# A graph layer's edge sums on one core: shorter packing sums, a share of the gathers fetched row by row from two hardware queues, PSUM copies moved to VectorE

## The chip, the cores and the metric

The kernel runs on one core of a Trainium2 chip, as a single program. The metric is the device time of one execution in microseconds. A profile is one further execution, recorded by the hardware profiler; its span runs from the first to the last instruction.

Engines are named as in the profile: PE (TensorE), PEld (its weight loads), DVE (VectorE), ACT (ScalarE), POOL (GpSimd), SP (SyncE). "SPq" and "ACTq" are what the sequencers of SP and ACT do themselves, issuing transfers and loading registers.

## The reference, cut to what matters

A layer over a graph of 50,000 nodes and 1,650,000 edges (src, dst), sorted by dst. Each node has 160 float32 features, each edge four numbers. Every node also has an edge to itself.

```python
ss, vv = s[src], v[src]                    # the features of the source node of each edge: 64 + 32 x 3
dot  = einsum('eui,ei->eu', vv, e1)
out0 = C0 * (ss * e0 @ W1 + dot * INV3 @ W2)
...
m     = concatenate([out0, out1], 1)       # a message for each edge
m_agg = segment_sum(m, dst, n)             # summed at the target node
h     = [m_agg_s @ Ws, m_agg_v @ Wv]       # 160 features again
y     = x + relu(h)
out   = layernorm(x + y)
```

All of a message is linear in (edge number k) x (source feature). So the kernel sums, for each target node and each k, the source rows weighted by the edge's number k, and applies the weights afterwards, per node.

## The kernel before, in words

**Units, groups, pairs.** 128 edges are a unit. G = 6 units are a group; as the edges are sorted by dst, the targets of a group lie in a window of W = 32 nodes. For a unit, POOL gathers the 128 source rows from HBM with one indirect DMA into a tile `xg` (`gather`, pool `rows`, six buffers). DVE builds from the targets a one-hot matrix `hot` and multiplies it by the four edge numbers to `ha`, 128 edges x (4 x 32) (`spread`). PE multiplies the two into PSUM `ps` (`group_sums`), six units per group. PG = 2 groups are a pair, and the main loop runs over the 1,050 pairs. SG = 20 groups are a superchunk: src, dst and the edge numbers of the next one are fetched (`load`), converted to float (`cast`) and transposed by PE (`place`) while the present one is worked on.

**After the sums.** Four groups are a chunk: `turn` transposes its sums on PE and copies them out of PSUM (`at`), `apply_weights` multiplies by the folded weights (`hp`), and `nodes`, `block` and `norm1` to `norm3` add up the chunks of 128 nodes, add x, normalize and store `out`. Copies from PSUM go through a name `evict`, which is ACT's copy here. These steps are put into the main loop a few pairs after the sums that they need (`after_pair`).

**Packing.** Each node has an edge to itself, so about one edge in 33 needs no gather from far: its source row lies in the group's own window. For 1,980 of the 2,100 groups (all but a head of NH = HEAD = 100 groups and a rest of 20), a group spans L = 787 edges, and K = 19 edges that loop onto their own node are taken out, so that 768 remain to be gathered. `pack` does this for RP = 120 groups at a time, one group per partition, with DVE:
- it marks the self edges (`m`), numbers them (`cum`) and computes how far each later edge moves up (`far`),
- it sums, for each window node w and edge number k, what the self edges carry (`waste`, with the sum in `mine`): 2 halves x 4 x 32 instructions over some 393 columns each,
- it moves the edges up in steps of 1, 2, 4, 8, 16, with predicated copies, and stores the result to HBM (`sd`, `ad`), from where `load` reads it.

`pack` is a generator: a step is taken at each pair, so that the work is spread up to the pair by which it must be done. What the self edges carry is added in `group_sums`: `own` fetches the 32 rows of the group's window four times over (`xo`, a transfer at an address loaded into a register), and DVE adds xo x `taken` to `ps` on its way to `A`.

**Fetching by rows.** The code has a second way to fill a unit, switched off in this kernel (`HELP = {}`). `fetch` loads row addresses (`offsets`, from a tile `ro`) into registers of SP or ACT and issues one transfer of 640 bytes for each row, into a tile `xr` (pool `far`, three buffers for each queue). `HELP` gives for each queue the number of units out of which it takes one. `batches` spreads the 128 rows in batches of ROWS over the pairs, the last two pairs ahead of their use; `gather` leaves out the units so filled, which come last in their pair.

**Queues.** SP's queue issues all loads and `own`; ACT's queue issues the weights and the stores of `out`.

Of the kernel before, what the change touches and what calls it, by code (L numbers as in the profile page):

```python
# [44 lines left out]
P = 128  # L45
# [17 lines left out]
HELP = {}  # L63
HEAD = 100
RP = 120
ROWS = 32
# [28 lines left out]
def tile_gnn_resnorm(ctx: ExitStack, tc: tile.TileContext, x, src, dst, attr, W1, W2, W3, W4, W5, Ws, Wv, out, n_edges):  # L95
# [92 lines left out]
    def norm3(pool, y, mv, rstd, n, row):  # L188
        nc.vector.reciprocal(rstd[:n], rstd[:n])  # L189
        o = pool.tile([P, D], F32, name="o")  # L190
        nc.vector.tensor_scalar(o[:n], y[:n], mv[:n, 0:1], rstd[:n], op0=ALU.subtract, op1=ALU.mult)  # L191
        nc.scalar.dma_start(out[row, :], o[:n])
# [18 lines left out]
    with tc.tile_pool(name="once", bufs=1) as once, tc.tile_pool(name="raw", bufs=2) as rawp, \  # L211
            tc.tile_pool(name="idx", bufs=2) as idxp, tc.tile_pool(name="rows", bufs=6) as rowp, \
            tc.tile_pool(name="far", bufs=3) as farp, tc.tile_pool(name="own", bufs=4) as ownp, \
# [13 lines left out]

        offsets = {}
        evict = nc.vector.tensor_copy if ET.Activation in HELP else nc.scalar.copy

        def load(s):
# [4 lines left out]
            if NH <= g0 < NH + NPK:  # L236
                sd, ad = stored[(g0 - NH) // RP]
                e = slice((g0 - NH) % RP * G * P, ((g0 - NH) % RP * G + n) * P)
                rf = rawp.tile([P, 2, P], F32, name="rf")
                for i in range(2):  # L240
                    nc.sync.dma_start(rf[:n, i, :], sd[i:i + 1, e].rearrange("o (u p) -> (o u) p", p=P))
                nc.sync.dma_start(ra[:n].rearrange("u p k -> u (p k)"), ad[e].rearrange("(u p) k -> u (p k)", p=P))
                return s, n, None, rf, ra
            e = slice(start(g0), start(g0) + n * P)
            ri = rawp.tile([P, 2, P], I32, name="ri")
            nc.sync.dma_start(ri[:n, 0, :], src1[e].rearrange("(u p) o -> u (p o)", p=P))
            nc.sync.dma_start(ri[:n, 1, :], dst1[e].rearrange("(u p) o -> u (p o)", p=P))
            nc.sync.dma_start(ra[:n].rearrange("u p k -> u (p k)"), attr[e].rearrange("(u p) k -> u (p k)", p=P))
# [55 lines left out]

        def own(p):

            s, g, ng = pairs[p]
            if not NH <= g < NH + NPK:
                return
            _, at = nc.values_load_multi_w_load_instructions(  # L310
                baseO[0:1, g:g + ng], engines=[ET.SP], min_val=0, max_val=(N - W) * 4 * D,
                skip_runtime_bounds_check_because="an offset of a row of x")
            xo = ownp.tile([P, PG, D], F32, name="xo")
            for i, v in enumerate(at):
                nc.sync.dma_start(xo[:, i, :].bitcast(U8),
                                  xbytes[ds(v, W * 4 * D)].rearrange("(w f) -> w f", w=W).unsqueeze(0)
                                  .to_broadcast([NK, W, 4 * D]))
# [20 lines left out]
        owns, stored, taken = {}, {}, {}  # L338
        halves = ((0, L // 2), (L // 2, L))

        def pack(c):
# [9 lines left out]
            nc.sync.dma_start(pri[:n, 0, :], src1[e].rearrange("(r e) o -> r (e o)", e=L))  # L351
            nc.sync.dma_start(pri[:n, 1, :], dst1[e].rearrange("(r e) o -> r (e o)", e=L))
            nc.sync.dma_start(pra[:n].rearrange("r e k -> r (e k)"), attr[e].rearrange("(r e) k -> r (e k)", e=L))
            nc.sync.dma_start(pb[:n], base_d[NH + r0:NH + r0 + n])
            yield
            nc.scalar.copy(prs[:n], pri[:n])
# [3 lines left out]
            cum = packp.tile([P, L], F32, name="cum")  # L360
            far = packp.tile([P, L], I32, name="far")
            less = packp.tile([P, L], I32, name="less")
            carry = packp.tile([P, 1], F32, name="carry")
            pbf = packp.tile([P, 1], F32, name="pbf")
            mine = packp.tile([P, 2, NK * W], F32, name="mine")
            waste = packp.tile([P, L], BF16, name="waste")
            nc.vector.tensor_scalar(pbf[:n], pb[:n], float(N - W), None, op0=ALU.min)
            for h, (a, e) in enumerate(halves):
                q = slice(0, e - a)
                nc.vector.tensor_tensor(m[:, q], prs[:n, 0, a:e], prs[:n, 1, a:e], op=ALU.is_equal)  # L370
                nc.vector.tensor_tensor_scan(cum[:n, a:e], m[:, q], zeros[:n].to_broadcast([n, e - a]),
                                             carry[:n] if h else 0.0, op0=ALU.add, op1=ALU.add)
                nc.vector.tensor_copy(carry[:n], cum[:n, e - 1:e])
                yield

                nc.vector.scalar_tensor_tensor(m[:, q], cum[:n, a:e], float(K), m[:, q], op0=ALU.is_le, op1=ALU.mult)
                nc.vector.tensor_scalar(cum[:n, a:e], cum[:n, a:e], float(K), None, op0=ALU.min)
                nc.vector.scalar_tensor_tensor(far[:n, a:e], m[:, q], 0.0, cum[:n, a:e],
                                               op0=ALU.is_equal, op1=ALU.mult)
                yield  # L380
                nc.vector.tensor_scalar(cum[:n, a:e], prs[:n, 1, a:e], pbf[:n], None, op0=ALU.subtract)
                nc.vector.tensor_reduce(packed[:n, 0, 2 * c + h:2 * c + h + 1], cum[:n, a:e], axis=AX.X, op=ALU.min)
                nc.vector.tensor_reduce(packed[:n, 1, 2 * c + h:2 * c + h + 1], cum[:n, a:e], axis=AX.X, op=ALU.max)

                nc.vector.scalar_tensor_tensor(m[:, q], cum[:n, a:e], 1.0, m[:, q], op0=ALU.add, op1=ALU.mult)
                yield
                for k in range(NK):
                    for w in range(W):
                        nc.vector.scalar_tensor_tensor(waste[:n, a:e], m[:, q], float(w + 1), pra[:n, a:e, k],  # L389
                                                       op0=ALU.is_equal, op1=ALU.mult,  # L390
                                                       accum_out=mine[:n, h, k * W + w:k * W + w + 1])
                        if w % 4 == 3:
                            yield
            nc.vector.tensor_copy(counts[:n, c:c + 1], carry[:n])
# [6 lines left out]
            for b in range(K.bit_length()):  # L401
                d = 1 << b
                for a, e in halves:
# [3 lines left out]
                    if d * 2 <= K:  # L407
                        nc.vector.tensor_scalar(less[:n, a:e + d], far[:n, a:e + d], 0x7fffffff - d, None,
                                                op0=ALU.bitwise_and)
# [8 lines left out]
                    yield  # L418
            sd = dram.tile([2, n * G * P], F32, name=f"sd{c}")
            ad = dram.tile([n * G * P, NK], F32, name=f"ad{c}")  # L420
            for i in range(2):
                nc.sync.dma_start(sd[i:i + 1].rearrange("o (r e) -> (o r) e", e=G * P), prs[:n, i, :G * P])
            nc.sync.dma_start(ad.rearrange("(r e) k -> r e k", e=G * P), pra[:n, :G * P])
# [37 lines left out]
        def nodes(b):  # L461
# [4 lines left out]
            nc.sync.dma_start(xt[:nb], x[row, :])  # L466
# [20 lines left out]
        nbatch = P // ROWS  # L487
        batches, helped = {}, {}
        for h, (eng, period) in enumerate(HELP.items()):
            first = PG * G + h * period // 2  # L490
            while True:
# [13 lines left out]
        def fetch(p):  # L505
            for eng, h, q, s, u, i in batches.get(p, []):
                if i == 0:
                    fetched[q, h] = farp.tile([P, D], F32, name=f"xr{h}")
                xr = fetched[q, h]
                _, at = nc.values_load_multi_w_load_instructions(  # L510
                    offsets[s][u:u + 1, i * ROWS:(i + 1) * ROWS], engines=[eng], min_val=0, max_val=(N - 1) * 4 * D,
                    skip_runtime_bounds_check_because="an offset of a row of x")
                for j, v in enumerate(at):
                    r = i * ROWS + j
# [7 lines left out]
        with nc.allow_non_contiguous_dma(reason="one number of each group"):  # L522
            for g0, g1, size in ((0, NH, G * P), (NH, NH + NPK, L), (NH + NPK, NGP, G * P)):
                if g0 < g1:
                    e = slice(start(g0), start(g0) + (g1 - g0) * size)
                    nc.sync.dma_start(base_d[g0:g1], dst1[e].rearrange("(g e) o -> g (e o)", e=size)[:, 0:1])
        baseI = baseB.bitcast(I32)
        nc.sync.dma_start(baseI, base_d.rearrange("g o -> o g").to_broadcast([P, NGP]))
# [4 lines left out]
        zeros = once.tile([P, 1], F32, name="zeros")  # L533
        nc.vector.memset(zeros, 0.0)
# [3 lines left out]
        packed = once.tile([P, 2, max(2 * npacks, 1)], F32, name="packed")  # L538
# [19 lines left out]
        hps, parts, of_nodes, resid, rstds = {}, {}, {}, {}, {}  # L558
# [15 lines left out]
        def do_store(b):  # L574
            norm3(np_, *resid.pop(b), rstds.pop(b), *rows_of(b))
# [245 lines left out]
```

## Time and profile before

| what | value |
|---|---|
| time before, median of 3 runs | 15,898.52 us (15,871.31 to 15,898.71) |
| time of the profiled execution | 15,879.8 us |
| span of the profiled execution | 15,878.0 us |
| mean granted TensorE clock | 0.648 of full speed |
| POOL busy | 11,926.1 us, 75% |
| PE busy, PE weight loads | 11,902.0 us, 75%; 8,781.1 us, 55% |
| DVE busy | 7,960.7 us, 50% |
| ACT busy | 897.9 us, 6% |
| moved by DMA | 1,382 MB, 87 GB/s |

A row of the groups reads: line, engine, operation, out<-in with shapes, count, then busy time in us and mean ns of one, then the engine's idle time just before these instructions, and what ended most of it. "issue" there means that nothing that the profile shows was waited for. Register loads and moves and the issuing of transfers are not counted as busy; the view of a single line gives their durations as min/median/max in ns.

### The profile page before, as it was taken

Reading aid. Unit: us, or ns where it says so; the run is one execution under the profiler, and the core shown is the slowest. Engines: PE = TensorE matmul, PEld = TensorE weight load, DVE = VectorE, ACT = ScalarE, POOL = GpSimd, SP = SyncE. Lnnn points to the kernel's source line nnn. Section 1 sums busy time; section 2 is a strip of 40 time slices with the busy share of each in tenths; the row PEclk is TensorE's granted clock in tenths of the full one; section 3 lists DMA queues with packets and bytes.
Section 4 is the critical chain, followed back from the end, with each engine's and each line's share of the span. In section 5 each row is a group of like instructions: output and inputs, shape, how many; then the busy total and the mean of one; then the engine's idle time right before and its main releaser. Section 6 shows DMA issues by size and latency. Waiting matters only on the chain. (4 is left out here: it accounts for less than half of the span.)

```text
span 15878.0 us, 132047 instructions
## 1 busy us (share of the span) xinstructions
PE 11902.0 (75%) x43059; PEld 8781.1 (55%) x43060; DVE 7960.7 (50%) x17460; ACT 897.9 (6%) x2069; POOL 11926.1 (75%) x12611
## 2 busy tenths in 40 slices
PE   7677777777777777777777777777777777777777
PEld 4455555555555555555555555555555555555555
DVE  4565555545454554545454554545455454545422
ACT  0000000000000000000000000000000000000000
POOL 7677777777777777777777777777777777777776
PEclk7666666666666666666666666666666666666666
DMA  3333333333333333333333333333333333333332
GB/s 83 74 86 94 84 82 96 82 95 84 94 83 92 85 82 96 83 96 83 94 85 87 91 82 96 84 94 84 94 83 82 96 82 96 83 93 84 86 83 70
DMA packets 1040422, 1382.05 MB, mean 87 GB/s; under 512 B 233153, under 2 KB 813393, under 8 KB 1035641
## 3 DMA queue, kind: packets, MB, share of 16 engines
q0 software_dynamic: 604800, 1033.00, 26.9%
q1 hardware_dynamic: 378065, 307.98, 7.1%
q10 hardware_dynamic: 56864, 32.58, 0.7%
q8 instruction: 344, 5.64, 0.1%
q14 instruction: 349, 2.86, 0.1%
HBM read 1303.90 MB, written 68.75 MB: 86 GB/s over the span
## 5 line engine op out<-in xcount | busy, mean ns | idle before, releaser
L288 POOL DMA_INDIRECT xg<-in_x,si x12600 | 11924.5, 946 | 3917.0 <-issue 3527.0
L325 PE MATMUL ps<-xg,ha 128*128 128x160 f32 x25200 | 8037.7, 447 | 3686.5 <-DMA xg<-in_x,si 3640.6
L325 PEld LDWEIGHTS ps<-xg,ha 128*128 128x128 f32 x25200 | 5302.5, 266 | 6227.7 <-DMA xg<-in_x,si 6033.2
L334 DVE SCALAR_TENSOR_TENSOR A<-xo,taken,ps 128x160 f32<-128x160 f32 x1980 | 728.8, 377 | 7231.3 <-PE ps L325 7231.3
L389 DVE SCALAR_TENSOR_TENSOR waste<-marks,pra 120x393 bf16<-120x393 f32 (+3 forms) x4352 | 3652.5, 839 | 2.9
L300 DVE TENSOR_TENSOR ha<-hot,pk 128x1536 f32<-128x1536 f32 x1050 | 1830.2, 1744 | 284.1 <-PE ps L325 284.0
L480 PE MATMUL phb<-hp,hot 128*128 128x160 f32 x4544 | 1181.0, 433 | 56.2 <-ACT at L439 52.8
L480 PEld LDWEIGHTS phb<-hp,hot 128*128 128x128 f32 x4544 | 1066.4, 297 | 173.3 <-ACT at L439 172.2
L436 PE MATMUL pt<-ident,A 128*128 128x128 f32 (+1 forms) x4200 | 1051.7, 406 | 100.1 <-ACT hp L454 67.8
L450 PE MATMUL phc<-BWb,at 32*128 32x160 f32 x4200 | 1078.0, 404 | 0.0
L439 ACT COPY at<-pt 128x512 f32<-128x512 f32 (+1 forms) x1050 | 596.9, 579 | 6815.1 <-PE pt L436 6746.4
L450 PEld LDWEIGHTS phc<-BWb,at 32*128 32x128 f32 x4200 | 835.0, 253 | 196.3 <-issue 196.1
L450 PE MATMUL phc<-BWa,at 128*128 128x160 f32 x4200 | 922.6, 374 | 2.3 <-ACT at L439 2.0
L436 PEld LDWEIGHTS pt<-ident,A 128*128 128x128 f32 (+1 forms) x4200 | 700.7, 178 | 302.7 <-ACT hp L454 143.1
L450 PEld LDWEIGHTS phc<-BWa,at 128*128 128x128 f32 x4200 | 847.0, 255 | 35.3 <-ACT at L439 35.3
L297 DVE TENSOR_TENSOR hot<-bank,rel 128x384 f32<-128x384 f32 x1050 | 569.6, 544 | 0.3
L454 ACT COPY hp<-phc 128x160 f32<-128x160 f32 x525 | 153.3, 292 | 6230.2 <-PE phc L450 6171.5
L470 DVE TENSOR_TENSOR hot<-bank,rr 128x768 f32<-128x768 f32 (+2 forms) x391 | 358.8, 918 | 0.1
L389 DVE DVE_READ_ACCUMULATOR waste<-marks,pra 120x1 f32 (+1 forms) x4352 | 342.9, 79 | 0.0
L416 DVE COPY_PREDICATED pra<-marks,pra 120x1572 f32<-120x1572 int32 (+6 forms) x170 | 323.5, 1903 | 0.0
L176 DVE SCALAR_TENSOR_TENSOR y<-phb,xt 128x160 f32<-128x160 f32 x391 | 120.6, 308 | 195.6 <-PE phb L480 195.3
L414 DVE COPY_PREDICATED prs<-marks,prs 120x393 f32<-120x393 int32 (+6 forms) x340 | 181.3, 582 | 0.1
(98 smaller groups left out, 1610.1 us busy)
## 6 DMA issues: line engine op xcount, KB each, us to landing
xg<-in_x,si POOLq DMA_INDIRECT x12600
xo<-in_x SPq DMA_DIRECT2D x1980, 80.0 KB
xt<-in_x SPq DMA_DIRECT2D x390, 80.0 KB
out<-o ACTq DMA_DIRECT2D x390, 80.0 KB
ra<-ad SPq DMA_DIRECT2D x99, 240.0 KB
pra<-in_attr SPq DMA_DIRECT2D x16, 1475.6 KB
ad<-pra SPq DMA_DIRECT2D x16, 1440.0 KB
rf<-sd SPq DMA_DIRECT2D x198, 60.0 KB
```

The source lines that it names most:

```text
L288: nc.gpsimd.indirect_dma_start(out=xg[:, j, :], out_offset=None, in_=x, in_offset=bass.IndirectOffsetOnAxis(ap=placed[0][:, u + j:u + j + ...
L297: nc.vector.tensor_tensor(hot[:, :n], slotsP[:, 0:W].unsqueeze(1).to_broadcast([P, n, W]), rel[:, u:u + n].unsqueeze(2).to_broadcast([P, n ...
L300: nc.vector.tensor_tensor(ha[:, :n], hot[:, :n].unsqueeze(2).to_broadcast([P, n, NK, W]), pk[:, :, u:u + n].rearrange("p k u -> p u k").un ...
L325: nc.tensor.matmul(ps[:, j // G, :], ha[:, j].rearrange("p k w -> p (k w)"), xr, start=j % G == 0, stop=j % G == G - 1)
L334: nc.vector.scalar_tensor_tensor(A[:, i], xo[:, i], taken[r // RP][:, r % RP:r % RP + 1], ps[:, i], op0=ALU.mult, op1=ALU.add)
L389: nc.vector.scalar_tensor_tensor(waste[:n, a:e], m[:, q], float(w + 1), pra[:n, a:e, k], op0=ALU.is_equal, op1=ALU.mult, accum_out=mine[:n ...
L416: nc.vector.copy_predicated(pra[:n, a:e], mi[:, r].unsqueeze(2).to_broadcast([n, e - a, NK]), pra[:n, a + d:e + d])
L436: nc.tensor.transpose(pt[:f1 - f0, g, :], A[:, i, f0:f1], ident)
L439: evict(at[:, :, :ng].rearrange("f k g w -> f g k w"), pt[:f1 - f0, :ng].rearrange("f g (k w) -> f g k w", w=W))
L450: nc.tensor.matmul(ph[:ng * W], at[:, k, :ng].rearrange("f g w -> f (g w)"), bw[:, k, :], start=i == 0, stop=i == 2 * NK - 1)
L470: nc.vector.tensor_tensor(hot2[:, :len(cs)], slotsP.unsqueeze(1).to_broadcast([P, len(cs), P]), rr[:, :len(cs)].unsqueeze(2).to_broadcast( ...
L480: nc.tensor.matmul(ph[:nb], hot2[:r, i, :nb], hp[:r], start=i == 0, stop=i == len(cs) - 1)
```

## The change

Constants: `HELP` is switched on, SP takes one unit in 45 in batches of 32 rows, ACT's queue one in 90 in batches of 16; HEAD goes from 100 to 60, so that 2,020 groups are packed. With ACT in HELP, `evict` becomes DVE's copy. With SP in HELP, everything that SP issued before is issued by ACT's queue (`dq`), so that SP issues rows alone; `own` loads the addresses of five pairs at a time, and has five buffers. The store of `out` becomes a step of its own, a pair after its computation. In `pack`, the sum for window node w runs over those columns alone in which the targets of w can lie (L = 787 edges, 33 to a node; `early` and `late` are six standard deviations, and two checks are added at the end that no self edge lies outside); some tensor_scalar operations are replaced by forms with one operand in PSUM or two tensors; and there are empty steps after its loads and ahead of its stores. The program has 2,856 such sums in place of 4,352.

```diff
-HELP = {}
-HEAD = 100
+HELP = {ET.SP: 45, ET.Activation: 90}
+HEAD = 60
-ROWS = 32
+ROWS = {ET.SP: 32, ET.Activation: 16}
...
-            tc.tile_pool(name="far", bufs=3) as farp, tc.tile_pool(name="own", bufs=4) as ownp, \
+            tc.tile_pool(name="far", bufs=3) as farp, tc.tile_pool(name="own", bufs=5) as ownp, \
...
+        own_eng = ET.Activation if ET.SP in HELP else ET.SP
+        dq = nc.scalar if ET.SP in HELP else nc.sync
         offsets = {}
         evict = nc.vector.tensor_copy if ET.Activation in HELP else nc.scalar.copy
...
-                    nc.sync.dma_start(rf[:n, i, :], sd[i:i + 1, e].rearrange("o (u p) -> (o u) p", p=P))
+                    dq.dma_start(rf[:n, i, :], sd[i:i + 1, e].rearrange("o (u p) -> (o u) p", p=P))
...
+        OWN = 5
         def own(p):
...
-            _, at = nc.values_load_multi_w_load_instructions(
-                baseO[0:1, g:g + ng], engines=[ET.SP], min_val=0, max_val=(N - W) * 4 * D,
+            if p % OWN == 0:
+                g1 = min(g + OWN * PG, NH + NPK)
+                _, at = nc.values_load_multi_w_load_instructions(
+                    baseO[0:1, g:g1], engines=[own_eng], min_val=0, max_val=(N - W) * 4 * D,
...
+        degree = n_edges / N
+        late = 6 * math.sqrt(L) + 2 * degree
+        early = -6 * math.sqrt(L)
...
-                nc.vector.tensor_scalar(cum[:n, a:e], cum[:n, a:e], float(K), None, op0=ALU.min)
...
-                for k in range(NK):
-                    for w in range(W):
-                        nc.vector.scalar_tensor_tensor(waste[:n, a:e], m[:, q], float(w + 1), pra[:n, a:e, k],
+                for w in range(W):
+                    w0 = max(a, math.floor(degree * w + early))
+                    w1 = min(e, math.ceil(degree * w + late) + 1)
+                    for k in range(NK if w0 < w1 else 0):
+                        nc.vector.scalar_tensor_tensor(waste[:n, w0:w1], m[:, w0 - a:w1 - a], float(w + 1), pra[:n, w0:w1, k],
                                                        op0=ALU.is_equal, op1=ALU.mult,
                                                        accum_out=mine[:n, h, k * W + w:k * W + w + 1])
...
-                        nc.vector.tensor_scalar(less[:n, a:e + d], far[:n, a:e + d], 0x7fffffff - d, None,
-                                                op0=ALU.bitwise_and)
+                        nc.vector.tensor_tensor(less[:n, a:e + d], far[:n, a:e + d], mi[:, 0:e + d - a],
+                                                op=ALU.subtract)
...
+            nr = ROWS[eng]
             _, at = nc.values_load_multi_w_load_instructions(
-                    offsets[s][u:u + 1, i * ROWS:(i + 1) * ROWS], engines=[eng], min_val=0, max_val=(N - 1) * 4 * D,
+                    offsets[s][u:u + 1, i * nr:(i + 1) * nr], engines=[eng], min_val=0, max_val=(N - 1) * 4 * D,
...
+        def do_send(b):
+            nb, row = rows_of(b)
+            dq.dma_start(out[row, :], outs.pop(b)[:nb])
...
                     after_pair(p + 6, do_store, b)
+                    after_pair(p + 7, do_send, b)
```

## The prediction

> **What bounds the kernel now.** I read the page's engine table first (POOL 75%, PE 75%, DVE 50%, ACT 6%: no verdict), then the costliest groups, then POOL's stretch of the timeline, because an engine that is busy 75% can still never rest.
>
> ```profile
> span 15878.0 us, 132047 instructions
> PE 11902.0 (75%) x43059; PEld 8781.1 (55%) x43060; DVE 7960.7 (50%) x17460; ACT 897.9 (6%) x2069; POOL 11926.1 (75%) x12611
> ...
> L288 POOL DMA_INDIRECT xg<-in_x,si x12600 | 11924.5, 946 | 3917.0 <-issue 3527.0
> L325 PE MATMUL ps<-xg,ha 128*128 128x160 f32 x25200 | 8037.7, 447 | 3686.5 <-DMA xg<-in_x,si 3640.6
> ```
>
> The first group: 12,600 gathers, 946 ns each, and of the 3,917 us idle before them 3,527 us are "issue": POOL waits for nobody. The second: PE's idle time ahead of the edge matmuls ends with the landing of those gathers. The timeline of POOL alone shows the beat:
>
> ```profile
> 8012.42 0.95 POOL L288 DMA_INDIRECT xg<-in_x,si  x1 [0.30 <-issue]
> 8013.68 0.95 POOL L288 DMA_INDIRECT xg<-in_x,si  x1 [0.30 <-issue]
> 8014.93 0.94 POOL L288 DMA_INDIRECT xg<-in_x,si  x1 [0.30 <-issue]
> 8016.17 0.95 POOL L288 DMA_INDIRECT xg<-in_x,si  x1 [0.30 <-issue]
> ```
>
> One gather starts every 1.25 us. The gathers run from 7.6 us (first start) to 15,842.8 us (last start). 12,599 steps of 1.25 us are 15,749 us, so 86 us are real stalls, the largest one of 36.4 us (POOL's wait for si, L273). The last 35 us are the end of the kernel. So **the time is 7.6 + 1.25 us a gather + 86 + 35**, and the profiled run (15,879.8 us, 1.8 us outside its span) lies 18.7 us below the median of the runs, 15,898.5 us.
>
> Who feeds the new work? SyncE and ScalarE's queue show in no busy row; the single-line views give what they issue:
>
> ```profile
> L310 SPq TENSOR_LOAD <-baseO x990: 640/975/3587, 46.0 to 15623.3; - x198
> ...
> L315 SPq MOVE xo<-in_x x1980: 29/38/38, 46.9 to 15637.6; - x198
> L315 SPq DMA_DIRECT2D xo<-in_x x1980: 547/585/708, 47.0 to 15637.7; - x198
> ```
>
> These are min/median/max in ns: loading two addresses into registers takes 975, moving one into place 38, issuing the transfer of 128 rows 585. Between them the queue's timeline has gaps of 30 and 41 ns. Transfers with a fixed address are cheaper (the store of `out` 338 on ACT's queue, `ad` 317 on SP's).
>
> **What the Trainium skill says.** "DMA: Bandwidth & Descriptors", SWDGE vs HWDGE vs iDMA, says that GpSimd's transfers have their descriptors computed in software, those of SP and ACT in hardware, all on the same 16 DMA engines, so that spreading only saves issue time. Issue time is what POOL lacks here (946 ns and the gap), while the three data queues take 26.9, 7.1 and 0.7% of the 16 engines' span: it agrees. "Perfetto Trace Analysis", DMA Instruction — HWDGE, says that the descriptor generator is locked by one queue at a time; no row of before shows such a wait. "SBUF — State Buffer", Who interferes with whom, says that DVE's two-port modes lock GpSimd out, while a DVE operation with at most one SBUF input outside these modes, such as a copy from PSUM, does not; the gathers keep 946 ns (median) beside every DVE row, which agrees.
>
> **The change part by part.**
> 1. *Fewer gathers.* The program has 12,176 instead of 12,600: 418 units are fetched by rows (279 on SP, 139 on ACT), 6 disappear because HEAD 60 packs 40 more groups. 424 × 1.25 = −530 us, all on the path. New sum: 7.6 + 12,175 × 1.25 + 86 + 35 = 15,348 us, 15,350 as profiled run, **15,368 against the median**.
> 2. *SP's rows: 35,712 transfers of 640 B and 1,116 loads of 32 addresses*, nothing else in the loop. POOL spends 15,219 us on its part, so SP may take 15,219/1,116 = **13.6 us for a burst of 32**; the old time is reached at 14.2 us. A row costs MOVE 38 + gaps 71 + its issue. That issue is not in the trace: above it is bounded by the row-addressed transfer of 128 rows (585), below by nothing but the MOVE's 38. I take 280, somewhat under the cheapest fixed transfer (317), as one row has one descriptor to make. 32 × 0.389 = 12.4 us. A load of 32 is unseen too: two registers take 0.64 to 0.98, and "DMA: Bandwidth & Descriptors", Latency and other measured facts, calls 600 ns a floor that loading several amortizes; but "Runtime: NRT & Kernel Launch", Instruction fetch mechanics, has 200 ns a register, which would be 6.4 us. I take 1.0. Sum 13.4 us: 1,116 × 13.4 = 14,950 us, **hidden under POOL by 2%**, with `farp`'s three buffers to smooth it. This is the thin point. If it fails, what is late is the last unit of a pair, then PE, and after the six `rows` buffers POOL. The load waits for `ro`, which ACT scales one superchunk ahead; behind that wait stand only the queue's own rows.
> 3. *ACT's queue* takes 17,792 rows (× 0.389 = 6,920 us), 1,112 loads of 16 (× 0.8 = 890), the 2,020 own transfers moved from SP (× 0.694 = 1,400) with 202 loads of ten (200), and moved issues of `xt`, `out`, `rf`, `ra` and the packs (about 1,200 × 0.4 = 480) plus roots and casts (150): about 10,000 of 15,350 us. With a row at 585 it would be 13,500, with 200 ns a register 2,900 more than mine: under the span each, over it together. It loses 1,050 × 579 + 525 × 292 + 60 × 425 = 787 us of copies. Behind its waits (root for DVE's mv, `xo` for a free buffer) stand rows, which are due two pairs (30 us) later; 5 `own` buffers instead of 4 loosen one of them. Taken as 0, at most some 250 us: 17 packs that hand over late by two bursts of 7 us.
> 4. *DVE.* Out: 4,352 sums × (839 + 79) = −3,995 us. In: 2,856 sums over 213 columns on average, 0.5 us each by the 839 for 393 with a little fixed cost, + 79: +1,650. PSUM copies: 1,050 × 0.65 (hot, 384 columns in 544) + 525 × 0.35 (L334: 377 for 160) + 40 × 0.5 = +890. Bound rows of the packs 34 × 2.2 = +75. Total near 6,600, 43%: off the path either way, as DVE waits for PE 7,231 us at L334 alone. Its price is 0; a copy in DVE's queue may hold PE's psM buffer a microsecond longer, which PE's slack of 3,640 us absorbs.
> 5. *Pools, memsets, iota, the checks at the end*: under 2 us on POOL, 2 us in the tail, 0 taken. HEAD 60 gives the first pack 19 pairs (285 us) instead of 39; its DVE work is about 165 us beside some 100 of the loop, so it fits, but the 36 us stall after it may be 0 or 80.
>
> **The rivals.**
> A. *SP becomes the metronome* (slower). Decides from 14.2 us a burst. With fixed-address issue, 32 × (0.317 + 0.109) + 1 = 14.6 us gives 1,116 × 14.6 + 75 = 16,370 us; with the skill's 200 ns a register 12.4 + 6.4 = 18.8 us gives 21,060. For it: two registers at 975 against one at 0.29 to 0.5 us in the end checks (L667) looks linear, and SP and ACT share a descriptor generator. Against: a single row has 1/128 of the descriptors, and nothing in the trace charges a row so much.
> B. *Rows or packs on ACT come late* (near the old time). The `xo`, `rf` and `ad` transfers that SP issued at once stand behind bursts and roots. Each time PE starves longer than the gathers in hand cover, POOL stops. The price is open; 3.7 us on each of ACT's 139 units are 514 us and eat the gain: 15,880. Against: every wait has two pairs of lead.
> C. *No gain although fewer gathers* (15,898), PE being the true bound: spoken against by PE's waits for the gathers (3,640 us as PE, 6,033 at the weight load).
>
> **How the numbers follow.** Forecast (POOL's beat stays, rows hidden) 0.52, at 15,368; its own range is 15,260 (the 86 us of stalls gone, a little more) to 15,620 (item 3's bound). A 0.36: its ends are 15,870 and 27,000 us (10.6 us a load); some 0.22 of it below 17,400. B and C 0.12, a third each side and in the middle. Left out are about 0.04 below and 0.15 above 15,260 to 17,400. No change means within 0.2% (32 us), about what a measurement of this kernel can tell. Faster: 0.52 + 0.04 = 0.56; same 0.05; slower 0.34 + 0.05 = 0.39.
>
> **What would show it.** Right: gathers still start every 1.25 us, POOL waits stay "issue", the groups have 12,176 gathers, SP's row issues are below 0.32 us, its loads of 32 below 2 us, and SP shows long waits for free `xr` buffers. Wrong: PE or PEld waits for xr<-in_x in the list of waits, with POOL's "issue" turned into waits for PE; SP's bursts following each other without a rest, over 14 us each; or, for B, waits for xo, rf or the ACT queue's rows. DVE is right near 6,600 us busy.

## The result, and the profile after

The changed kernel takes **21,663.4 us** (median of 4 runs, 21,661.8 to 21,667.8) against 15,898.6: a ratio of **1.363 [1.361, 1.366]**. The forecast was 15,368, the range ended at 17,400. The first eight experiments (labels e and f) ran on chips on which SP's own instructions took far longer in stretches (in f4 one in nine of SP's MOVEs took some 0.7 us instead of 0.03, while a gather kept its 948 ns) and the kernel before took 19,048 and 18,921 us, so of these only the ratio to the kernel before of the same group is used.

The page after, in the rows that answer to those of before:

```profile
span 21660.2 us, 236086 instructions
PE 6734.2 (31%) x43039; PEld 6308.0 (29%) x43040; DVE 7268.1 (34%) x16264; ACT 194.0 (1%) x554; POOL 11540.8 (53%) x12188
...
L292 POOL DMA_INDIRECT xg<-in_x,si x12176 | 11538.5, 948 | 9996.4 <-issue 3554.7
L334 PE MATMUL ps<-xr,ha 128*128 128x160 f32 x836 | 304.9, 461 | 14136.3 <-DMA xr<-in_x 14080.4
```

The gathers kept their length (948 ns) and their gap (3,554.7 / 11,647 = 0.31 us), and there are 424 fewer. But POOL's idle time is 9,996 us now, not 3,917. The wait list (engine, line, what it waited for: total us, times, longest) says for whom:

```profile
PE ps L334 <- DMA xr<-in_x: 14080.4, 278, 73.5
...
POOL xg L292 <- issue: 3554.7, 11647, 0.6
POOL xg L292 <- PE pt L468: 3535.9, 132, 61.7
...
POOL xg L292 <- PE ps L334: 2845.5, 259, 51.5
```

POOL's new stalls are waits for PE, 3,535.9 + 2,845.5 = 6,381 us. They account for the loss: the gathers run from 19.3 us (first start) to 21,536.9 us (last start), of which 12,175 steps of 1.25 us are 15,219 us; the other 6,299 us are these stalls, less the 0.3 us that each of the 391 would have had as its gap (some 6,260 us). PE stands for `xr` 278 times, 50.6 us each. Matching the row matmuls of the trace with those of the program, one by one, gives whose rows they are: PE stands over 1 us at each of SP's 279 units and at none of ACT's 139. PE's timeline shows one such stand:

```profile
7971.68 0.43 PE L272 MATMUL bank<-ident,rf 120*128 120x120 f32 x2
8015.16 0.87 PE L334 MATMUL ps<-xr,ha 128*128 128x160 f32 x2 [43.06 <-DMA xr<-in_x]
8016.51 0.69 PE L468 MATMUL pt<-ident,A 128*128 128x128 f32 x2 [0.47 <-DVE A L343]
```

So the rows come late. Not because SP is slow at issuing them; the single-line views of the row transfers and of the register loads (min/median/max ns) are:

```profile
L548 SPq MOVE xr<-in_x x35712: 29/29/38, 11.3 to 21629.5; - x200
L548 SPq DMA_DIRECT2D xr<-in_x x35712: 14/208/2042, 18.2 to 21629.5; - x200
...
L548 ACTq DMA_DIRECT2D xr<-in_x x17792: 224/234/542, 46.6 to 21466.9; - x200
```

```profile
L543 SPq TENSOR_LOAD <-ro x1116: 2034/2172/4026, 9.2 to 21617.4; - x186
L543 ACTq TENSOR_LOAD <-ro x1112: 1199/1559/3915, 45.2 to 21458.2; - x186
```

A row costs 208 + 29 + 66 of gaps = 303 ns, a burst 32 × 0.303 + 2.17 = 11.9 us, below the 13.4 of the forecast. Nor do ACT's rows slow the issue: in h2 (below), where ACT fetches none, SP's median is 208 ns as well. What SP does besides is in the queue's own wait list:

```profile
SPq L548 <- DMA xr<-in_x: 5680.5, 5745, 71.3
SPq L548 <- DMA xo<-in_x: 976.6, 268, 50.1
...
SPq L548 <- PE ps L334: 14.4, 67, 0.3
```

SP waits for *transfers to land*: for `xr` rows (those of ACT and its own) and for `xo`, which is ACT's. It reads none of them. And it almost never waits for PE to free an `xr` buffer (14.4 us), so its three buffers are never all full.

**Where such a wait comes from** stands in the program as built. Every transfer of SP's and of ACT's queue signals one of eight completion semaphores, taken in turn *by both queues together*, in the order in which the scheduler laid the program out; before a transfer is issued, the one that had its semaphore before must have landed. One row of SP, and the transfer eight places ahead of it (uses of a semaphore counted in transfers):

```
SP   I-113962  row of xr0   semaphore 1, use 3449   waits: semaphore 1, use 3448
ACT  I-114898  xo           semaphore 1, use 3448   waits: semaphore 1, use 3447; DVE 6988 (an xo buffer free)
```

The numbers are the order of writing: this SP row waits for an `xo` written 936 instructions *later*. That `xo` waits for DVE to be done with the sums of a pair (I-114314), and PE starts on this pair only after the matmul that uses SP's unit before (I-113887). So the ring is closed: the row cannot start until PE has used the last unit that SP fetched. Over all SP rows that follow an ACT transfer the median is +1,124, five pairs (about 224 instructions a pair); the last of a unit's rows are written only two pairs ahead of their use. Matched with the trace in the same way, 5.9 ms of SP's waits are behind transfers of ACT and 1.7 ms behind SP's own rows.

An account by queue carries the rest. **Work** is the durations of SP's instructions and the first 60 ns of every gap between them, **waits** are all that lies beyond, in ms, summed over the records of each trace. The last two columns are PE's idle time just before the row matmuls of SP's and of ACT's units, in ms, with the number of units at which it is over 1 us:

| kernel | SP rows every | time, us | ratio | SP work | SP waits | PE at SP's units | PE at ACT's units |
|---|---|---|---|---|---|---|---|
| changed kernel | 45 | 21,663 | 1.363 | 13.86 | 7.80 | 14.14 (279 of 279) | 0 (0 of 139) |
| g1: order alone changed | 45 | 20,510 | 1.291 | 13.91 | 6.54 | 2.82 (131 of 279) | 4.08 (139 of 139) |
| h1: rows in turn | 45 | 18,312 | 1.153 | 13.95 | 4.36 | 3.13 (140 of 279) | 3.55 (139 of 139) |
| i2: rows in turn, SP's begun earlier | 45 | 18,330 | 1.152 | 13.88 | 4.41 | 0.24 (58 of 278) | 3.62 (139 of 139) |
| h2: SP's rows alone, order as built | 45 | 18,725 | 1.179 | 13.63 | 5.09 | 11.21 (279 of 279) | none |
| j1: SP's rows alone, order changed | 45 | 16,296 | 1.027 | 13.74 | 2.49 | 4.39 (254 of 279) | none |
| i4: rows in turn | 54 | 16,944 | 1.065 | 11.65 | 5.27 | 4.22 (206 of 232) | 2.05 (122 of 139) |
| h4: order as built | 80 | 15,521 | 0.977 | 8.14 | 7.39 | 0.12 (7 of 157) | 0.13 (32 of 139) |

The work always fits under POOL's 15.4 ms, and at one unit in 45 it hardly changes while the time goes from 21.7 to 16.3 ms, so the time is not made by SP's issuing. Work and waits add up to the span by definition: a wait in this account is any time without work, harmful or not, as h4's 7.39 ms show. What is late is told by the columns on PE.

### The profile page after: what moved, and what is told of

The parts are those of the page before. It is cut to its first block, busy times and chain, and to the rows that moved or that the text cites. A ratio compares the mean times of both kernels' runs of the same rounds, so it can differ in the third digit from the quotient of the medians.

```text
span 21660.2 us, 236086 instructions
## 1 busy us (share of the span) xinstructions
PE 6734.2 (31%) x43039; PEld 6308.0 (29%) x43040; DVE 7268.1 (34%) x16264; ACT 194.0 (1%) x554; POOL 11540.8 (53%) x12188
## 5 line engine op out<-in xcount | busy, mean ns | idle before, releaser
L292 POOL DMA_INDIRECT xg<-in_x,si x12176 | 11538.5, 948 | 9996.4 <-issue 3554.7
L334 PE MATMUL ps<-xr,ha 128*128 128x160 f32 x836 | 304.9, 461 | 14136.3 <-DMA xr<-in_x 14080.4
L334 PE MATMUL ps<-xg,ha 128*128 128x160 f32 x24352 | 4003.4, 326 | 77.6 <-DVE A L339 52.6
L334 PEld LDWEIGHTS ps<-xg,ha 128*128 128x128 f32 x24352 | 3826.2, 212 | 189.4 <-issue 63.9
L343 DVE SCALAR_TENSOR_TENSOR A<-xo,taken,ps 128x160 f32<-128x160 f32 x2020 | 654.0, 376 | 9085.8 <-PE ps L334 9062.3
L419 DVE SCALAR_TENSOR_TENSOR waste<-marks,pra 120x236 bf16<-120x236 f32 (+45 forms) x2856 | 1498.2, 525 | 92.0
L468 PE MATMUL pt<-ident,A 128*128 128x128 f32 (+1 forms) x4198 | 704.7, 306 | 609.8 <-DVE A L343 542.7
L471 DVE COPY at<-pt 128x512 f32<-128x512 f32 (+1 forms) x1050 | 668.7, 678 | 376.6 <-PE pt L468 287.9
L482 PE MATMUL phc<-BWb,at 32*128 32x160 f32 x4200 | 709.4, 307 | 0.0
L512 PE MATMUL phb<-hp,hot 128*128 128x160 f32 x4538 | 681.8, 299 | 0.0
L512 PEld LDWEIGHTS phb<-hp,hot 128*128 128x128 f32 x4538 | 638.4, 190 | 0.7 <-DVE at L471 0.5
```

The lines of the kernel that those rows point to most:

```text
L292: nc.gpsimd.indirect_dma_start(out=xg[:, j, :], out_offset=None, in_=x, in_offset=bass.IndirectOffsetOnAxis(ap=placed[0][:, u + j:u + j + ...
L334: nc.tensor.matmul(ps[:, j // G, :], ha[:, j].rearrange("p k w -> p (k w)"), xr, start=j % G == 0, stop=j % G == G - 1)
L343: nc.vector.scalar_tensor_tensor(A[:, i], xo[:, i], taken[r // RP][:, r % RP:r % RP + 1], ps[:, i], op0=ALU.mult, op1=ALU.add)
L419: nc.vector.scalar_tensor_tensor(waste[:n, w0:w1], m[:, w0 - a:w1 - a], float(w + 1), pra[:n, w0:w1, k], op0=ALU.is_equal, op1=ALU.mult, a ...
L468: nc.tensor.transpose(pt[:f1 - f0, g, :], A[:, i, f0:f1], ident)
L471: evict(at[:, :, :ng].rearrange("f k g w -> f g k w"), pt[:f1 - f0, :ng].rearrange("f g (k w) -> f g k w", w=W))
```

## The experiments

**e1: no rows at all** (all else of the change stays, but the PSUM copies stay on ScalarE and the loads on SP).
```diff
-HELP = {ET.SP: 45, ET.Activation: 90}
+HELP = {}
```


> The changed kernel with HELP = {}: no unit is fetched by rows; SyncE issues the transfers again and ScalarE copies out of PSUM. The shorter packing sums, HEAD = 60, the grouped own loads and the later store stay. Every theory: 12,594 gathers at 1.25 us plus about 130 us of start, stalls and end, 15,870 us, within 0.5% of the kernel before. If it is over 16,500, something other than the rows costs the time.

Measured: ratio 1.0027 [1.0003, 1.0051]. HEAD, the windows of the sums and the packs cost nothing that matters; the loss comes with the rows, or with the copies and loads that moved because of them. The latter are cleared by h4 below, which has both and is faster than the kernel before.

**e2, e3, e5: other HELP**, {SP: 45}, {SP: 60, ACT: 90}, {SP: 80, ACT: 90}, the first with the copies kept on VectorE.

> HELP = {SP: 45} alone: ScalarE's queue fetches no rows, but still issues all other transfers, and the PSUM copies stay on VectorE. Theory L (lockstep: the transfers of both queues take their completion semaphores in turn from one set of eight, and each waits for the one eight places ahead in the scheduler's order; in that order SyncE's rows stand behind own transfers of ScalarE's queue that are later in the program, so that SyncE can start a unit only when the one before has been consumed): SyncE's rows still stand behind later own transfers (1,762 of them in the built program), so the time stays far above: 279 units at 65 to 78 us, 18,100 to 21,700 us. Theory A (ScalarE's queue is late with its own rows): without them 12,315 gathers at 1.25 + 130 = 15,520. Theory R (each row costs a fixed 0.118 us of the whole, 6,310 us over 53,504 rows): 15,520 + 35,712 x 0.118 = 19,730.

> HELP = {SP: 60, ACT: 90}: SyncE has 72.9 us for a unit and needs 4 x 11.9 = 47.6 us of issuing. Theory L: the order in the built program is still the wrong way round (SyncE's rows wait for transfers of ScalarE's queue that are a median of 839 instruction numbers later in the program), so a unit takes the 77.6 us of the changed kernel: 209 units, 16,200 to 16,600 us. Theory I (SyncE's bare issue speed): hidden, 12,245 gathers, 15,440. Theory A: unchanged ScalarE rows, above 20,000. Theory R: 15,440 + 44,500 x 0.118 = 20,690.

> HELP = {SP: 80, ACT: 90}: in the built program SyncE's rows now wait for transfers of ScalarE's queue that are a median of 415 instruction numbers earlier in the program, not later. Theory L: the lockstep is harmless, rows are hidden, 12,297 gathers at 1.25 + 130 = 15,500 us, below the kernel before by 2.4%. Theory A: above 20,000, ScalarE's rows are as many as before. Theory R: 15,500 + 37,900 x 0.118 = 19,970. Theory I: 15,500 as well.

Measured: 1.563 [1.559, 1.569], 1.359 [1.354, 1.364], 1.111 [1.109, 1.113], where the changed kernel (f4, below) has 1.573. Taking ACT's rows away changed next to nothing on these chips (h2 repeats it); fewer SP rows took off more than their share, 0.36 and 0.11 of excess where 45/60 and 45/80 of 0.573 would be 0.43 and 0.32. L's numbers (18,100 to 21,700, then 16,200 to 16,600, then 15,500 us where the kernel before takes 15,900) were missed in all three.

**f1 to f4, and g1.** In f1 and g1 the order alone changes, the instructions are those of the changed kernel. Each transfer of ACT is ordered, without a wait, behind the last SP row written ahead of it:
```diff
+            def dma_start(self, *args):
+                made = nc.scalar.dma_start(*args)
+                if behind:
+                    tc.add_manual_dep(made.ins, behind[-1].name, ...)  # NoSync
...
```
f2 is e5 once more.


> The changed kernel, the same instructions; only the order in which the program is laid out is different: every transfer of ACT's queue that is written after a burst of SP stands behind that burst when the eight completion semaphores are dealt out (an order without a wait of its own). In the changed kernel an SP row that follows an ACT transfer in the row of semaphores follows one that is written 1,124 instructions later (median); here one that is written 130 earlier. Theory L (SP's rows wait, through the shared semaphores, for ACT transfers that themselves need PE to have used SP's last unit): SP gets its lead back, PE's waits for xr shrink from 14,080 us to under 1,000, and the time falls to 15,350 to 15,900 where the kernel before takes 15,900 (ratio 0.965 to 1.0). Theory I (SP's issue of single rows is too slow, or the rows hold up the transfers of POOL): nothing changes, ratio 1.36. Theory M (ACT's queue is so full that its own rows or own transfers come late): the ratio stays above 1.1, and the waits for ACT's rows or xo lead the list.

> The changed kernel with SP fetching one unit in 80 instead of 45, all else as it is. Its first run, beside a kernel before of 19,048 us, had a ratio of 1.111. Theory L: at 80 the order laid out is already the right way round (ACT's transfers written 415 instructions before the SP rows that follow them in the row of semaphores), so most of the excess goes: 15,500 to 16,200 us, ratio 0.975 to 1.02. If rows cost time by contention (theory C), the excess of 5,765 us shrinks in proportion to SP's rows, 45/80: 0.56 of it stays, about 19,100 us, ratio 1.20. Theory I says much the same as L here, since SP is used less; the run with the order alone changed tells those two apart.

f3 fetches `xo` once and uses it for all pairs, so it leaves out the own rows of each pair. f4 is the changed kernel.

> The changed kernel with the own rows (xo) fetched once ahead of the loop and used by all pairs: it leaves out the own rows of each pair and so 2,020 transfers and 202 register loads of ACT's queue. These are the ACT transfers that wait for PE's last pair through a free xo buffer. Theory L in its narrow form (xo closes the ring): the lockstep is broken, ratio below 1.05. Theory L in its wide form (any ACT transfer laid out ahead of its turn closes it: out, xt, rf wait for DVE and PE too): the time falls little, ratio 1.2 to 1.35. Theory I: ratio 1.36.

> The changed kernel once more, beside the others on one chip, to set them against: ratio 1.36 to the kernel before, and PE's waits for xr near 14,080 us in 278 waits.

Measured: f1 1.510 [1.507, 1.512], f2 1.109 [1.107, 1.111], f3 1.563 [1.559, 1.566], f4 1.573 [1.569, 1.577]. On these chips the order helped a little. `xo` alone is not the link that closes the ring: in f3 PE still stood 268 times for `xr`. g1 is f1 once more, beside a kernel before at 15,886 us:

> The kernel with the order alone changed, once more. Beside the first such run, on a chip where the kernel before took 18,921 us, every engine's instructions came slower in stretches (SP's MOVE 0.7 us instead of 0.03), so that SP had no rest at all and its own pace set the time: 28,544 us, against 29,772 of the changed kernel. Where the kernel before takes its usual 15,900 us, SP's work for a unit is 47.6 us of 56: theory L then gives a ratio of 0.965 to 1.0, theory I (SP's pace is the bound whatever the order) 1.36.

20,510 us, 1.291 [1.282, 1.300]: against 21,663 some 1,150 us less, so L missed its numbers by far. SP's waits:

```profile
SPq L559 <- DMA xr<-in_x: 3601.5, 3116, 97.5
SPq L559 <- DMA xo<-in_x: 2318.7, 1879, 4.6
```

The `xo` wait went from 268 long waits (3.6 us mean) to 1,879 of 1.2 us. The order did what it was meant to for SP's units: PE stands at 131 of 279 of them now, for 2.8 ms instead of 14.1. But it stands at every one of ACT's, for 4.1 ms, where it stood at none: theory M, that ACT's own rows come late, holds here. Why the two hold each other up is a reading, tested by h1: with whole bursts behind each other in the row of eight, the queues pass the turn to one another instead of working side by side.

**h1: rows in turn; h2: SP alone; h3: ACT alone; h4: one in 80.** h1 is g1 with the rows of an SP and an ACT burst of the same pair written alternately, two to one. h2 is e2, h4 is e5. h3:
```diff
+HELP = {ET.Activation: 60}
```


> The changed kernel, the same instructions, with the order of the one before (ACT's transfers behind the SP bursts written ahead of them) and the rows of an SP burst and of an ACT burst of one pair laid out in turn, two to one, instead of one burst behind the other. Theory S (the eight shared completion semaphores let neither queue run more than eight transfers ahead of the other in the order laid out, so that with whole bursts standing behind each other SP's 13.4 ms and ACT's some 9.8 ms of issue add up instead of lying beside each other): the two now run side by side; SP's waits for ACT's transfers fall from 6,300 to under 2,500 us, and the time to 15,400 to 16,500 us (ratio 0.97 to 1.04). Theory M (ACT's queue itself is late, stuck behind its waits for DVE): stays above 19,500 (1.23).

> The changed kernel with SP's rows alone, one unit in 45, in the order as built; ACT fetches no unit, and keeps the own rows and the moved loads. Theory S: SP 13.4 ms and ACT about 2.2 ms make 15.6 ms: 15,500 to 17,000 us, ratio 0.98 to 1.07. Theory L (SP's rows stand behind later ACT transfers that wait for PE to use SP's last unit, one unit per turn): 20,000 us or more, 1.26 upwards, with 279 waits of PE for xr.

> The other queue alone: ACT fetches one unit in 60 (209 units) in bursts of 16, SP keeps own rows and loads, all other edits as in the changed kernel. 12,385 gathers. ACT's rows are some 11.4 ms of issue, SP's transfers 2.5 ms. Theory S: their sum of 14 ms lies under POOL's 15.5: 15,898 - 215 x 1.25 = 15,630 us, 15,600 to 15,800, ratio 0.981 to 0.994. Theory L: SP's own transfers wait for PE, and ACT's rows fall into the same lockstep: ratio above 1.05.

> SP one unit in 80, ACT one in 90, as built, once more beside the others. Theory S: 157 units are 7.5 ms of SP, with ACT's 9.8 ms 17.3 ms less what the eight in flight overlap (23.2 ms became 21.66 in the changed kernel): about 16,000 us, ratio 0.99 to 1.05. Theory C (the rows cost the other transfers their time, in proportion to their number): 1.20.

h1 1.153 [1.151, 1.155], a large step, but short of what S gave (SP's waits behind ACT's transfers fell from 6.2 to 3.1 ms, not under 2.5); h2 1.179 [1.177, 1.181], between S and L; h3 1.026 [1.023, 1.028], over S's numbers and under L's, and the queue that carries the rows is ACT here, with 11.9 ms of work and 4.47 of waits; h4 **0.977 [0.975, 0.979]**, better than S gave. PE's waits for rows in h1, h2 and h3, one fence each:

```profile
PE ps L345 <- DMA xr<-in_x: 4297.3, 180, 59.6
```

```profile
PE ps L334 <- DMA xr<-in_x: 11210.1, 279, 81.7
```

```profile
PE ps L334 <- DMA xr<-in_x: 8903.7, 207, 73.1
```

Where the order is as built (h2, h3), PE stands for nearly every unit (279 of 279 and 207 of 209): the lockstep of the changed kernel, with either queue. With the order changed (h1) it stands less often, at half of SP's units but still at all of ACT's. h4's page has the forecast's picture:

```profile
span 15536.8 us, 202987 instructions
...
L292 POOL DMA_INDIRECT xg<-in_x,si x12298 | 11661.8, 948 | 3808.2 <-issue 3584.3
L334 PE MATMUL ps<-xg,ha 128*128 128x160 f32 x24596 | 6440.9, 405 | 2702.6 <-DMA xg<-in_x,si 2413.2
...
L334 PE MATMUL ps<-xr,ha 128*128 128x160 f32 x592 | 202.2, 444 | 241.7 <-DMA xr<-in_x 195.2
```

POOL waits for next to nobody again, PE waits for the gathers, and is idle for 242 us ahead of the row matmuls where it was for 14,136. 7.6 + 12,297 × 1.25 + 35 = 15,414, and 123 us of stalls make the 15,537: 302 gathers fewer than before are 378 us, 355 were measured. SP's waits are no shorter than in the changed kernel:

```profile
SPq L548 <- DMA xo<-in_x: 2426.3, 1408, 38.3
SPq L548 <- DMA xr<-in_x: 2329.6, 4639, 102.0
SPq L548 <- DMA out<-o: 1467.8, 171, 39.1
```

Two things differ: in this layout an SP row follows an ACT transfer written 415 instructions *earlier* (median), and SP has 8.1 ms of work where it had 13.9. Which of the two makes the waits harmless isn't separated.

**i1 to i4: what is left of 18,312?** i1 and i2 begin SP's rows three pairs earlier, in the order as built and with rows in turn; i3 moves root, store and sending of a block two pairs later, with rows in turn; i4 is h1 with SP: 54.
```diff
-                q = at[-1] + 2
+                q = at[-1] + (5 if eng == ET.SP else 2)
```


> The changed kernel, order as built, with SP's rows begun three pairs earlier (a unit is used five pairs after its last burst instead of two; the same three buffers). Theory L (a ring: SP's row waits for an ACT transfer, that for PE, PE for SP's last unit): what counts is how far SP's rows stand behind in the order laid out against how early they are wanted. The order laid out has SP 1,747 instructions behind now, 1,124 before, so the three pairs (some 230 instructions each) are just eaten: 20,500 to 21,700 us, ratio 1.29 to 1.37. If a lack of time between issue and use were the cause, the time would fall below 18,000.

> Rows of SP and ACT laid out in turn (18,312 us) and SP's rows begun three pairs earlier. Theory L: with the order right, three more pairs (45 us) open the ring: ACT's stands (10,050 us at the root for DVE's mv) no longer reach PE, and the time is SP's 13.4 ms of work with some 3 ms of short waits beside it, 15,500 to 16,900 us, ratio 0.975 to 1.065. Theory T (SP has no rest anyway: 13.4 ms of issue and 4.4 ms of waits for landings and for ACT make the 18.3 ms): the same 18,000 to 18,400 us, ratio 1.13 to 1.16.

> Rows laid out in turn, and ACT's root, the store and the sending of a block two pairs later, so that ACT's queue stands less at the root for DVE's mv (10,050 us before, 229 times). Theory M (these stands of ACT's queue are what SP waits for, 2,109 us behind ACT's rows): SP's waits fall by about 2,000 us and the time to 16,000 to 16,800 us, ratio 1.01 to 1.06. Theory T: at most 500 us, ratio 1.12 or more; ACT then stands at another wait.

> Rows laid out in turn with SP fetching one unit in 54 (233 units; 12,222 gathers). Theory T (time = SP's work and waits, 65.6 us a unit when laid out in turn): 233 x 65.6 = 15,290 us, which just goes under POOL's 15,450: 15,400 to 15,800 us, ratio 0.97 to 0.995. Theory L (each unit costs a ring's turn whatever the number): the excess of 18,312 over 15,400 shrinks in proportion, 233/279, to 2,430: 17,800 us, ratio 1.12.

i1 1.345 [1.341, 1.350], inside L's numbers: the earlier start is eaten by the layout. i2 1.152 [1.150, 1.154], i3 1.142 [1.140, 1.144], as T gave, and neither shortens SP's waits (4.41 and 4.22 ms after 4.36). But in i2 T hit the number without its reason, that SP has no rest: with more lead SP's units come in time (PE stands at 58 of 278, for 0.24 ms in all), and PE stands at each of ACT's 139 for 26 us, 3.62 ms in all. ACT's rows kept their two pairs of lead; beginning these earlier too wasn't tried. i4 1.065 [1.063, 1.067] lies between T and L: the work fell by 2.3 ms as it should, but the waits grew from 4.36 to 5.27, those behind ACT's rows from 2.1 to 3.2. Why they grew is open; that they did speaks against a fixed wait for each unit, which T had assumed.

**j1: h2 with the order changed.** Same instructions, no rows on ACT.

> SP's rows alone, one unit in 45, ACT fetching none, the instructions of the run with SP's rows alone (18,725 us, ratio 1.179); only the order laid out is changed: ACT's own rows, loads and stores stand behind the SP bursts written ahead of them, where before an SP row stood behind ACT transfers written 885 instructions later. Theory T with the order (SP's own work is 13.7 to 13.9 ms and goes under POOL's 15.5 if nothing but landings has to be waited for): SP's waits fall from 5,090 to under 2,300 us, and the time to 15,500 to 16,200 us, ratio 0.975 to 1.02. Theory R (SP's waits for xo are landings of 80 KB transfers just issued, whatever the order): SP's waits stay at 3,500 us or more, and the time at 17,200 to 18,700 us, ratio 1.08 to 1.18.

16,296 us, 1.027 [1.025, 1.028]; T's numbers ended at 16,200 and at 2,300 us of waits, R's began at 17,200. SP's waits of h2, then of j1:

```profile
SPq L548 <- DMA xo<-in_x: 3107.7, 1642, 60.3
SPq L548 <- DMA pb<-base_d: 482.1, 16, 70.5
SPq L548 <- DMA sd<-prs: 444.6, 24, 44.9
```

```profile
SPq L559 <- DMA out<-o: 986.4, 56, 47.9
SPq L559 <- DMA xo<-in_x: 951.7, 560, 30.4
```

2,429 us are won with the same instructions on the same engines, by the order in which they are laid out. SP's and POOL's instructions stand in one order in both built programs. ACT's don't, as was meant; but PE's and DVE's have moved as well (by 4 and 244 places, median), so it isn't shown that the turn of the semaphores alone won all of it. What speaks for the semaphores is the list: SP's waits fell by 2.6 ms, those for `xo` from 3.1 to 0.95. What stays is for `out` and `xo` in about equal parts, up to 48 us at a time. PE still stands at 254 of the 279 units, 17 us each instead of 40.

## Why the prediction was wrong, point by point

1. *Fewer gathers*: right. 12,176 gathers at an unchanged beat; h4, with 12,298, landed where this sum puts it.
2. *SP's rows: here it failed.* In sum the sizes were on the safe side, by two misses that partly cancel: a row took 0.303 us for 0.389, a load of 32 registers 2.17 for 1.0, a burst 11.9 for 13.4. The failed step is its last sentence, "behind that wait stand only the queue's own rows", and with it "hidden under POOL by 2%, with `farp`'s three buffers to smooth it". Ahead of an SP row stands, through the shared semaphores, whatever either queue has eight places earlier. SP's total was 13.86 ms of work *and 7.80 ms of waits* where the step had 14.95 and none, and the buffers smoothed nothing, as SP never filled them. That SP's rows then come late is shown by PE's stands, 14.1 ms at SP's units and none at ACT's; that the order laid out makes the difference, by h2 against j1 and by the changed kernel against g1.
3. *ACT's queue*: its work was near the 10,000 us worked out (8,998 us of instructions, some 10,700 with the gaps of up to 60 ns), and well under the span. This is luck in part: a load of 16 took 1.56 us for 0.8, a row 0.234 to issue for 0.28. One bound was mis-added, too: with 585 ns for the issue of a row the queue would take 15,470 us, not 13,500, and that alone is over the span. "Taken as 0, at most 250 us" asked only whether ACT would be late for its own readers. In the changed kernel it wasn't, and what it cost was SP; with the order changed (g1, h1, i2) it is, at every one of its units, for 3.6 to 4.1 ms. g1, h1 and j1 take 20.5, 18.3 and 16.3 ms, and between the last two ACT's rows are the main difference.
4. *DVE*: 7,268 us for 6,600. The copies measured 712 + 170 = 882 us (890 given), the sums 1,498 and their reads 236 (1,650 for both). Most of the gap is arithmetic: DVE's records overlap, those of before add up to 9,252 us where the page counts 7,961 as busy, and the forecast took 3,995 us of record lengths off the 7,961. In record lengths it would have been 7,872 us; 8,016 were measured. DVE was off the path, as given: DVE waits 9,062 us for PE at L343.
5. *Pools, HEAD, the end*: right as far as e1 reaches.

Of the rivals, A named 21,060 us, close to the time, for a reason that did not happen: bursts of 18.8 us from slow loads. B had the right kind of cause (ACT's queue holds things up) but passed it through the readers of ACT's data, and priced it at 3.7 us a unit. Of the signs listed, those of "wrong" came (PE's waits for `xr`, POOL's idle time gone over to PE), but not bursts of over 14 us of issue; of those of "right" the row's 208 ns came and the load of under 2 us didn't; and the sign "long waits for free `xr` buffers" was the one to look for: 14 us.

Open stays what would bring ACT's rows in time once the order is changed. The wait list of h1 has 10,050 us ahead of the root for DVE's `mv`, but these are idle time of ScalarE, in which its queue goes on issuing rows; the queue itself stands 1.6 ms at the root, so i3 could move only little (1.6 ms there too). Of the 7.7 ms that ACT's queue waits in all in h1, trace and program matched as above put 4.0 at rows that have a transfer of SP's ahead of them on their semaphore, and 1.4 at rows that have one of its own. Of SP's 4.4 ms 1.2 are behind SP's own rows and 3.1 behind ACT's transfers, 2.1 of these behind its rows. So more than half of each queue's waits still stand behind the other queue. That a set of semaphores for SP alone would end the waits wasn't tried.

The version to keep is h4, one unit in 80 on SP: 15,521 us, 2.3% faster than the kernel before (15,876 us beside it).

## What to carry to other kernels

When work is given to an idle queue, count what its instructions take and then ask what each must wait for that is not its data: completion semaphores, shared in turn between queues as in this program, tie a queue to the slowest thing that the other one waits for. In no order tried did SP carry such waits with 13.6 to 13.9 ms of work in some 15.4; with 8.1 ms, and another order, it did. Look at the queue's own wait list first: waits for transfers that it doesn't read, and none for a free buffer, mean that it never gets ahead. And when one queue's rows have been put right, see whose rows the engine waits for then: here they were the other queue's, and the time stayed.

## What the runs showed of the hardware

- A transfer of a single row of 640 B takes 208 ns to issue on SP and 234 on ACT, against 552 (ACT, after) and 585 (SP, before) for 128 rows at an address in a register, all medians: one row is far from 1/128 of it. From the start of its issue to the end of its last packet it takes 0.96 us (median over SP's queue, 1.9 us for one in twenty), so with eight in flight SP's rows, 0.3 us apart, seldom wait for one another: 0.08 ms in all in j1. Beside ACT's rows they do so more, 1.7 ms in the changed kernel.
- Register loads are neither flat nor linear in their number: two registers 0.98 us (before, SP), ten 1.91, sixteen 1.56 (both ACT, after), 32 2.17 (SP, after). The 200 ns a register that the Trainium skill has in "Runtime: NRT & Kernel Launch", Instruction fetch mechanics, for loads that its terms describe as coming from HBM, would give 6.4 us for 32; here they come from a tile on the chip, and the measurement decides.
